# Attention's output projection for two tiles at once, as seven block products with streamed weights

## The chip, the core and the metric

The kernel runs on one core of a Trainium2 chip. The metric is the device time of one launch in microseconds (us); lower is better. All data are f32.

## The reference

The reference is four layers of a small network on `x`, 64 sequences of 32 positions with 512 features (2048 rows). The change touches the attention of the third layer only. Cut to that:

```python
q = rope(rmsnorm(x @ Wq.T)) ; k = rope(rmsnorm(x @ Wk.T)) ; v = x @ Wv.T   # 32 query heads, 8 key heads, 128 wide
k_all = concat(k_cache[pages], k) ; v_all = concat(v_cache[pages], v)      # 512 cached + 32 own positions
probs = softmax(where(valid, q @ k_all.T / sqrt(128), -1e30))
o = (probs @ v_all).reshape(64, 32, 32 * 128)
return o @ Wo.T                                                            # 4096 -> 512
```

The last line is what is computed in another way: for all 2048 rows, a product of a 2048 x 4096 matrix with a 4096 x 512 matrix.

## The kernel before, in words

The kernel runs layer 0 (`layer0`), layer 1 (`layer1`), and then `attention`, whose end (`Tail.run`) is the rest of layers 2 and 3. Attention goes over **32 steps**: two halves of the heads (`HALVES`, 16 query heads and 4 key heads each), and in each half 16 tiles of 128 rows, which are four sequences of 32 positions. A step has 16 **turns** (`per`), one for each sequence and key head. In a turn TensorE transposes the probabilities of the turn (`turned`), computes the scores of two turns later (`start`, `scores`, L791), and multiplies values by probabilities (`values`, tile `po`). VectorE and ScalarE do the softmax of a turn (L796 mask, scale and maximum; L798 exponential; L800 reciprocal; L803 division), so that the result is there two turns on.

The other work on TensorE stands in **slots**, two in each turn (0 to 31), written out by hand. These are the projections of the next step (`Projection.product`: keys `pk`, values `pv`, four groups of queries `pq`, each in two parts; then `turned`, the transposes after the rotation) and the output product of the step before (`Output.product`, tile `py`). The order of TensorE is that of the program text (`on_pe`); the orders of the other engines and of the DMA queue of SyncE (SP) are laid out by a scheduler from the same text. POOL adds and multiplies in the rotation (L694, L695) and issues the gathers of values (`load_values`, L662); SP issues the keys, 16 pages of 64 KB for each sequence (`load_keys`, `load_by` L98), whose page numbers it reads from DRAM into registers (`numbers`, L93).

A tile's heads are collected in `oT` (128 x 16 heads x 128 positions), which `own_part` fills for two sequences at a time (L839). The output product of a tile is 16 matmuls, one for each head of the half, with `oT` as weights and 512 columns of `wo` moving, in eight blocks of two matmuls in slots 18 to 31 (1 to 15 in the last step). The weights `wo` of a half (16 x 512 per partition, 32 KB) stay in SBUF. VectorE takes the sum out of PSUM (L768; in the second half L770 adds `y_before`, what the first half has left in DRAM). PSUM tiles of projections and outputs share the tag `mm` with two buffers; the small transposes share `tq` with one. The weights of the second half are loaded in steps 14 and 15 (`weights`, `output_weights`). After the last step the last tile's output product stands alone, and then `Tail.run` begins.

Of the kernel before, what the change touches and what calls it, by code (L numbers as in the profile page):

```python
# [60 lines left out]
class Common:  # L61
# [26 lines left out]
    def numbers(self, src, n):  # L88


        nc = self.nc
        with self.tc.issue_after(self.last_load) if self.last_load else nullcontext():
            _, values = nc.values_load_multi_w_load_instructions(  # L93
                src, engines=[mybir.EngineType.SP], min_val=0, max_val=n - 1)
        return values

    def load_by(self, dst, src):
        self.last_load = self.nc.sync.dma_start(dst, src).ins  # L98
# [458 lines left out]
class Known:  # L557


    def __init__(self, c, kp):  # L560
        tc, nc, a = c.tc, c.nc, c.a
        half = HD // 2
        with tc.tile_pool(name="l2_setup", bufs=1) as scratch:
# [10 lines left out]
            for h in range(HALVES):  # L574
                t = kp.tile([P, B * L // P], I32, name=f"v_rows{h}")
                nc.vector.tensor_scalar(t, rows_f, float(h), None, ALU.add)
                self.rows.append(t)
            lens_i = c.load(scratch, "lens", [P, B], a["lens"].to_broadcast([P, B]), I32)
# [13 lines left out]
def attention(c, known, x_in, y_part, y_out, tail):  # L592
# [13 lines left out]
    with ExitStack() as outer:  # L606
# [14 lines left out]
              "q": wp.tile([P, KC, HQP * HD], F32, name="wq"),  # L621
              "o": op.tile([P, HQP, D], F32, name="wo")}
# [21 lines left out]
        kts = {}  # L644
# [4 lines left out]
        def load_keys(h, b):  # L649
            pages = c.numbers(a["pages"][0:1, b * NPP:(b + 1) * NPP], PAGES)  # L650
            for n in range(NPP):
# [46 lines left out]
        class Projection:  # L698


            def __init__(self, h, T, w):
                self.h, self.T, self.w = h, T, w
                self.r, self.acc = {}, {}

# [19 lines left out]
            def product(self, what, u):  # L724

                n, g = (what, 0) if what in ("k", "v") else ("q", what)
                if what == "v" and u == 0:
# [23 lines left out]
        class Output:  # L751


            def __init__(self, h, T, oT, w):
                self.h, self.T, self.oT, self.w = h, T, oT, w

            def product(self, u):
                if u == 0:
                    self.acc = ps.tile([P, D], F32, tag="mm", bufs=2, name="py")
                    if self.h:  # L760
                        self.before = c.load(wk, "y_before", [P, D], y_part(self.T))
                part(self.acc, [(self.oT[:, n, :], self.w["o"][:, n, :]) for n in (2 * u, 2 * u + 1)],
                     u == 0, u == HQP // 2 - 1)
                if u < HQP // 2 - 1:
                    return
                y = wk.tile([P, D], F32, name="y")
                if self.h == 0:
                    nc.vector.tensor_copy(y, self.acc)  # L768
                else:
                    nc.vector.tensor_tensor(y, self.acc, self.before, ALU.add)  # L770
                self.y = y

            def store(self):
                nc.sync.dma_start((y_out if self.h else y_part)(self.T), self.y)
# [69 lines left out]
        def weights(h, what):  # L844
# [4 lines left out]
            nc.sync.dma_start(ws[n][:, :, g * D:(g + 1) * D],  # L849
                              a[f"W{n}T"][:, at:at + D].rearrange("(k p) n -> p k n", p=P))  # L850

        def output_weights(h, u):

            at = (h * HQP + 4 * u) * HD
            nc.sync.dma_start(ws["o"][:, 4 * u:4 * (u + 1), :],
                              a["WoT"][at:at + 4 * HD].rearrange("(n p) o -> p n o", p=P))
# [13 lines left out]
        def keys_of(i):  # L870
            if i < len(turns):
# [3 lines left out]
                load_keys(h, b)  # L875
# [16 lines left out]
        oTs, stores = {0: qp.tile([P, HQP, P], F32, name="oT")}, []  # L892
# [34 lines left out]
        with tc.issue_after(c.last_load):  # L927
            for u in range(HQP // 4):
                output_weights(0, u)
        for s, (h, T) in enumerate(steps):  # L930
            if s:
                oTs[s] = qp.tile([P, HQP, P], F32, name="oT")
            slots = [[] for _ in range(2 * per)]
            if s == 0:
                slots[0].append(partial(projections[0].turned, 2))
                slots[2].append(partial(projections[0].turned, 3))
                slots[2].append(partial(own_keys, 0, 1, projections[0].kT))
            if s + 1 < len(steps):
                p = projections[s + 1]
                for what, at in zip(("v", "k") + GROUPS,  # L940
                                    ((1, 2), (3, 4), (6, 7), (8, 10), (11, 13), (14, 16))):
# [388 lines left out]
```

## Time and profile before

| what | us |
|---|---|
| median of 3 runs (lowest to highest) | 3682.45 (3680.71 to 3685.24) |
| profiled execution, its own time | 3681.84 |
| its span, first to last instruction | 3679.8 |
| TensorE (PE) busy / weight loads (PEld) busy | 3631.7 / 2523.7 |
| VectorE (DVE) / ScalarE (ACT) / GpSimd (POOL) busy | 1805.6 / 1316.3 / 1254.1 |
| attention's steps, about | 1081 to 3495 |
| a step in the middle (32 of them) | about 73 |

The page gives busy times and the chain of work that ended last, followed back from the last instruction. Other views answer queries on the same execution: the waits of an engine (who waited for whom: us in total, times, longest), the chain in order of time (start, length, what), the timeline of an engine, groups of instructions, and windows (busy time of every engine in a stretch). PE records two entries for each f32 matmul. A busy record of PE can overlap the next, so paces are read from the chain in order of time or from starts in the timeline.

### The profile page before, as it was taken

How to read it: one execution, taken by the hardware profiler on the slowest of the kernel's cores; microseconds unless marked ns; L12 is line 12 of the kernel's file. 1: busy time of each engine (PE TensorE's matmuls, PEld its weight loads, DVE VectorE, ACT ScalarE, POOL GpSimd, SP SyncE). 2: the span in 40 equal slices, each digit the busy share in tenths (PEclk: the TensorE clock that was granted, in tenths of full speed). 3: DMA queues.
4: the chain of work that ended last, by engine and by line, in shares of the span. 5: the costliest groups of instructions: out<-in, count | busy, mean ns of one | idle time of the engine just before them, and what ended most of it. 6: DMA issues, size and time to landing. Idle time of an engine off the chain costs nothing.

```text
span 3679.8 us, 62184 instructions
## 1 busy us (share of the span) xinstructions
PE 3631.7 (99%) x18752; PEld 2523.7 (69%) x18752; DVE 1805.6 (49%) x4815; ACT 1316.3 (36%) x3014; POOL 1254.1 (34%) x1265
## 2 busy tenths in 40 slices
PE   8999999999999999999999999999999999999999
PEld 3444788888867776777777776777777777777755
DVE  5452222222236655565556655566555655566423
ACT  1111111111125444444444444444444444444411
POOL 0112100000035444544445444444444444454222
PEclk9999999999999999999999999999999999999999
DMA  5014211111144444344443355544444344444521
GB/s 209 23 35 162 92 44 60 44 47 34 37 141 134 124 122 122 117 116 116 123 122 118 115 184 179 165 132 119 123 123 125 117 123 122 129 120 123 160 68 61
DMA packets 410062, 407.70 MB, mean 111 GB/s; under 512 B 49954, under 2 KB 322338, under 8 KB 409730
## 3 DMA queue, kind: packets, MB, share of 16 engines
q1 hardware_dynamic: 363010, 251.65, 22.5%
q0 software_dynamic: 44416, 147.88, 13.2%
q10 hardware_dynamic: 2304, 4.20, 0.3%
q8 instruction: 153, 2.51, 0.3%
q14 instruction: 179, 1.47, 0.1%
HBM read 382.57 MB, written 20.97 MB: 110 GB/s over the span
## 4 chain that ended last, share of the span: by engine, by line
PE 89%; SPq 1%; DMA 0%; DVE 0%; issue 0%; ACT 0%; POOL 0%; ACTq 0%; POOLq 0%; DVEq 0%
PE po L640 14%; PE sc L791 13%; PE pq L640 12%; PE py L640 12%; PE gate_up L311 10%; PE prT_ps L635 6%; PE pz L311 5%; PE po L1100 3%; PE pv L640 3%; PE pk L640 3%; PE po L311 2%; PE qkT_ps L635 2%; PE pd L247 1%; PE ph L122 1%; SPq L93 0%
## 5 line engine op out<-in xcount | busy, mean ns | idle before, releaser
L662 POOL DMA_INDIRECT vt<-in_v_rows,v_rows x512 | 500.7, 978 | 816.7 <-PE po L640 708.8
L640 PEld LDWEIGHTS po<-prT,vt 128*128 128x128 f32 x4096 | 530.1, 192 | 183.7 <-issue 178.0
L796 DVE CUSTOM_DVE_ANT_0 pr<-sc,mask 128x544 f32<-128x544 f32 x512 | 369.2, 721 | 458.7 <-PE sc L791 457.5
L798 ACT ACTIVATE pr<-pr,low 128x544 f32<-128x544 f32 x512 | 383.4, 749 | 540.7 <-DVE low L796 536.4
L791 PE MATMUL sc<-kt,qT 128*128 128x288 f32 (+1 forms) x2048 | 555.1, 394 | 5.2 <-ACT qT L748 2.4
L640 PE MATMUL po<-prT,vt 128*128 128x128 f32 x4096 | 540.8, 275 | 1.6 <-ACT prT L809 1.6
L791 PEld LDWEIGHTS sc<-kt,qT 128*128 128x128 f32 x2048 | 369.2, 191 | 180.8 <-issue 106.9
L640 PE MATMUL py<-wo,oT 128*128 128x512 f32 x1024 | 480.3, 593 | 0.7 <-ACT oT L839 0.7
L640 PE MATMUL pq<-wq,xT 128*128 128x512 f32 x1024 | 480.9, 593 | 0.0
L809 ACT COPY prT<-prT_ps 128x512 f32<-128x512 f32 x512 | 298.5, 583 | 272.6 <-PE prT_ps L635 269.4
L803 DVE TENSOR_SCALAR pr<-pr,low 128x512 f32<-128x512 f32 x512 | 364.5, 712 | 16.7
L635 PE MATMUL prT_ps<-ident,pr 128*128 128x128 f32 x2048 | 310.9, 275 | 1.3 <-DVE pr L803 1.3
L640 PEld LDWEIGHTS py<-wo,oT 128*128 128x128 f32 x1024 | 192.6, 191 | 137.5 <-issue 125.6
L640 PEld LDWEIGHTS pq<-wq,xT 128*128 128x128 f32 x1024 | 182.8, 191 | 129.9 <-issue 125.1
L800 DVE RECIPROCAL low<-low 128x1 f32<-128x1 f32 x512 | 83.5, 163 | 360.6 <-ACT pr L798 359.6
L635 PEld LDWEIGHTS prT_ps<-ident,pr 128*128 128x128 f32 x2048 | 237.7, 141 | 9.1 <-issue 1.5
L126 POOL TENSOR_TENSOR rs<-rs,minus_half 128x4 f32<-128x4 f32 x160 | 166.2, 1039 | 167.4 <-DVE rs L678 166.1
L694 POOL TENSOR_TENSOR rot<-rot,swapped 128x512 f32<-128x512 f32 x160 | 202.7, 1267 | 1.0
L801 ACT ACTIVATE own_pr<-pr,low 128x32 f32<-128x32 f32 x512 | 164.2, 321 | 106.3 <-DVE low L800 104.2
L695 POOL TENSOR_TENSOR rot<-rot,rs 128x512 f32<-128x512 f32 x160 | 177.1, 1107 | 8.0
L395 DVE TENSOR_TENSOR sg<-sg,gate_up 128x256 f32<-128x256 f32 (+1 forms) x88 | 37.1, 421 | 277.3 <-ACT sg L394 277.3
L677 DVE TENSOR_REDUCE rs<-squares 128x4 f32<-128x512 f32 x160 | 109.6, 685 | 118.9 <-ACT squares L675 116.3
(208 smaller groups left out, 4649.8 us busy)
## 6 DMA issues: line engine op xcount, KB each, us to landing
kt<-in_kT SPq DMA_DIRECT2D x2048, 64.0 KB
xt<-x SPq DMA_DIRECT2D x48, 256.0 KB
wq<-in_WqT SPq DMA_DIRECT2D x12, 1024.0 KB
A<-in_A SPq DMA_DIRECT2D x64, 152.0 KB
sets<-in_cond0T SPq DMA_DIRECT2D x32, 256.0 KB
vt<-in_v_rows,v_rows POOLq DMA_INDIRECT x512, 3.7
wo<-in_WoT SPq DMA_DIRECT2D x8, 1024.0 KB
y<-y SPq DMA_DIRECT2D x32, 256.0 KB
```

The costliest lines, as they stand in the source:

```text
L126: self.nc.gpsimd.tensor_tensor(t, t, self.minus_half[:, :n], ALU.pow)
L311: c.on_pe(nc.tensor.matmul(out, lhsT, rhs, start=start, stop=stop))
L635: c.on_pe(nc.tensor.transpose(pt[:, m, :], piece, c.ident))
L640: c.on_pe(nc.tensor.matmul(out, lhsT, rhs, start=first and i == 0, stop=last and i == len(pairs) - 1))
L662: nc.gpsimd.indirect_dma_start(out=vts[b % 2][:, n, :], out_offset=None, in_=a["v_rows"], in_offset=bass.IndirectOffsetOnAxis(ap=rows[h][: ...
L694: nc.gpsimd.tensor_tensor(r, r, tmp, ALU.add)
L695: last = nc.gpsimd.tensor_tensor(r, r, rs.unsqueeze(2).to_broadcast([P, REP, HD]), ALU.mult)
L791: c.on_pe(nc.tensor.matmul(sc[:, lo + n * PSIZE:lo + m * PSIZE].rearrange("p (n k) -> p n k", k=PSIZE), q, kt[:, n:m, g, :], start=True, s ...
L796: nc.vector.tensor_tensor_reduce(pr[:, :NK], sc[:, lo:lo + NK], masks[h, b], -SCALE, 3.0e38, ALU.add, ALU.min, low[:, 0:1])
L798: nc.scalar.activation(pr[:, :NK], pr[:, :NK], AF.Exp, bias=low[:, 0:1], scale=-1.0, accum_out=low[:, 1:2])
L803: nc.vector.tensor_scalar(pr[:, :L], pr[:, :L], low[:, 2:3], None, ALU.mult)
L809: nc.scalar.copy(prT, pt)
```

## The change

The output of two neighbouring tiles is formed together. Let the tiles' rows be A1 and A2 (`oT` of two steps), each cut in its heads: 8 heads and 8 heads, so that A is 2 x 2 blocks of 128 rows x 1024. `Wo` of the half is cut in 2 x 2 blocks of 1024 x 256. Instead of eight block products, seven are computed, from sums and differences of blocks (Winograd's form of Strassen's scheme), and y is put together from the seven:

- Sums of blocks of `Wo` (four for each half) are made by VectorE in steps 0 and 1 (`sum_up`), and stored in DRAM (`sums`).
- Sums of blocks of `oT` are made for each pair: two by POOL (`first_sums`, 1024 elements each; by VectorE after the last step), two by VectorE in place between products (`next_sum`, in halves of 512).
- Weights come in pieces of 128 x 4 x 256 (0.5 MB), 14 for a pair, through four buffers (`wo_tile`, `wo_piece`, `next_wo`); the load of a piece is put into the slot after the block that released its buffer (`later`).
- A product has two blocks of 4 matmuls with 256 columns. A pair has 14 blocks, spread over the slots of the two steps that follow the pair; steps 0 and 1 have none, and the last pair's stand after the last step.
- The projections' slots are spread anew, with two plans (even and odd steps), and values come last in odd steps. In steps 14 and 15 the loads of the second half's weights move one slot.
- `oT` has three buffers, and `oTs` of a pair are kept until its products are done. y is put together by ScalarE (2 copies of 256), VectorE (5 additions of 256) and POOL (2 additions of 256, in the second half 2 of 512 with `y_before`).
- The page numbers are put into a table in SBUF once, held between their bounds there (`Known.pages`); `numbers` reads them from it, and the bounds are not looked at again on SP. A sequence's keys are issued in four parts over three slots.

The diff, cut to its core:

```diff
     def load_by(self, dst, src):
-        self.last_load = self.nc.sync.dma_start(dst, src).ins
+        with self.tc.issue_after(self.last_load) if self.last_load else nullcontext():
+            self.last_load = self.nc.sync.dma_start(dst, src).ins
...
-        def load_keys(h, b):
-            pages = c.numbers(a["pages"][0:1, b * NPP:(b + 1) * NPP], PAGES)
-            for n in range(NPP):
+        def load_keys(h, b, parts=range(4)):
+            if 0 in parts:
+                pages[:] = c.numbers(
+                    known.pages[b:b + 1, :], PAGES,
+                    skip_runtime_bounds_check_because="Known holds them between the bounds")
+            for n in range(parts[0] * NPP // 4, (parts[-1] + 1) * NPP // 4):
                 c.load_by(kts[h, b][:, n, :], a["kT"][ds(pages[n], 1), h].rearrange("a d f -> (a d) f"))
...
+        H = D // 2
+        KH = HQP // 2
+        QH = KH // 2
+        ORDER = (1, 2, 5, 6, 7, 3, 4)
+        ahead = 4
+        def wo_tile():
+            return op.tile([P, QH, H], F32, name="wo", bufs=ahead)
+        def sum_up(h, k):
+            w, t = [], []
+            def rows():
+                w.append(wo_tile())
+                for n in range(2):
+                    at = (h * HQP + n * KH + k) * HD
+                    c.load_by(w[0][:, 2 * n:2 * n + 2, :].rearrange("p a b -> p (a b)"),
+                              a["WoT"][at:at + HD, :])
+            def add():
+                t.append(wo_tile())
+                (b11, b12, b21, b22), (t1, t2, t3, t4) = ([v[0][:, n, :] for n in range(4)] for v in (w, t))
+                nc.vector.tensor_tensor(t1, b12, b11, ALU.subtract)
+                nc.vector.tensor_tensor(t3, b22, b12, ALU.subtract)
+                nc.vector.tensor_tensor(t2, b22, t1, ALU.subtract)
+                nc.vector.tensor_tensor(t4, b21, t2, ALU.subtract)
+            def store():
+                c.load_by(sums[h][:, k], t[0])
...
+        class Outputs:
...
+            def first_sums(self, engine):
+                self.o = [oTs.pop(2 * self.n + i) for i in range(2)]
+                (_, _), (o21, o22) = self.blocks = [(o[:, :KH, :], o[:, KH:, :]) for o in self.o]
+                self.s = qp.tile([P, KH, P], F32, name="o_sum", bufs=1)
+                engine.tensor_tensor(self.s, o21, o22, ALU.add)
+                engine.tensor_tensor(o21, self.blocks[0][0], o21, ALU.subtract)
+            def next_sum(self, m, u):
...
+                if m == 6:
+                    nc.vector.tensor_tensor(self.s[:, q], self.s[:, q], o11[:, q], ALU.subtract)
+                else:
+                    nc.vector.tensor_tensor(self.s[:, q], o12[:, q], self.s[:, q], ALU.subtract)
...
+            def product(self, i):
+                m, u = ORDER[i // 2], i % 2
...
+                if u == 0:
+                    self.acc = ps.tile([P, D], F32, tag="mm", bufs=2, name="py")[:, :H]
+                (o11, o12), (o13, o22) = self.blocks
+                lhs = {1: o11, 2: o12, 3: self.s, 4: o22, 5: self.s, 6: self.s, 7: o13}[m]
+                w = wos.pop(0)
+                part(self.acc, [(lhs[:, u * QH + n, :], w[:, n, :]) for n in range(QH)], u == 0, u == 1)
...
+        def slot(fs):
+            now = later[:]
+            del later[:]
+            for f in now[:2]:
+                f()
+            later[:] = now[2:]
+            for f in fs:
+                f()
...
-                for what, at in zip(("v", "k") + GROUPS,
-                                    ((1, 2), (3, 4), (6, 7), (8, 10), (11, 13), (14, 16))):
+                if s == 0:
+                    plan = (("v", 1, 2), ("k", 4, 6), (0, 8, 10), (1, 13, 16), (2, 17, 20), (3, 22, 25))
+                    then = (12, 16, 20, 25, 29)
+                elif s == 1:
+                    plan = (("k", 1, 3), (0, 5, 8), (1, 10, 12), (2, 16, 17), (3, 19, 21), ("v", 24, 27))
+                    then = (10, 13, 19, 24, 28)
+                elif even:
+                    plan = (("v", 1, 2), ("k", 3, 5), (0, 6, 8), (1, 9, 11), (2, 12, 13), (3, 15, 16))
+                    then = (10, 13, 17, 19, 21)
+                else:
+                    plan = (("k", 2, 4), (0, 5, 6), (1, 8, 9), (2, 11, 13), (3, 19, 20), ("v", 22, 24))
+                    then = (10, 12, 16, 19, 27)
...
-                slots[28].append(projections[s + 2].x)
+                slots[29 if s < 2 else 26].append(projections[s + 2].x)
                 if steps[s + 2][0] != h:
-                    for what, at in zip(("v", "k") + GROUPS, (3, 5, 8, 11, 14, 17)):
+                    for what, at in zip(("v", "k") + GROUPS, (4, 6, 9, 12, 15, 18)):
                         slots[at].append(partial(weights, steps[s + 2][0], what))
...
+            if n == 0:
+                for k in range(KH):
+                    for f, at in zip(sum_up(s, k), (0, 7, 9)):
+                        to_come.setdefault(s * 2 * per + 4 * k + at, []).append(f)
+            else:
+                out = outputs[n - 1]
+                if even:
+                    slots[4].append(partial(out.first_sums, nc.gpsimd))
...
+                    ats = (17, 19, 24, 27, 29, 31, 33, 36, 39, 41, 44, 47, 49, 52) if last_pair else \
+                        (17, 19, 20, 22, 24, 25, 27, 29, 31, 33, 48, 49, 60, 62)
...
-        for u in range(HQP // 2):
-            out.product(u)
+        out = outputs[-1]
+        out.befores()
+        out.first_sums(nc.vector)
+        for i in range(n_out):
+            out.product(i)
+            next_wo()
+            if i in (5, 7):
+                for u in range(2):
+                    out.next_sum(6 if i == 5 else 3, u)
         out.store()
```

Numbers of blocks' slots above 31 lie in the step after (48 is slot 16 of the odd step).

## The prediction

> **What bounds the kernel now.** First the page's busy times, then its chain of work.
>
> ```profile
> PE 3631.7 (99%) x18752; PEld 2523.7 (69%) x18752; DVE 1805.6 (49%) x4815; ACT 1316.3 (36%) x3014; POOL 1254.1 (34%) x1265
> ...
> PE 89%; SPq 1%; DMA 0%; DVE 0%; issue 0%; ACT 0%; POOL 0%; ACTq 0%; POOLq 0%; DVEq 0%
> PE po L640 14%; PE sc L791 13%; PE pq L640 12%; PE py L640 12%; PE gate_up L311 10%; PE prT_ps L635 6%; PE pz L311 5%; PE po L1100 3%; PE pv L640 3%; PE pk L640 3%; PE po L311 2%; PE qkT_ps L635 2%; PE pd L247 1%; PE ph L122 1%; SPq L93 0%
> ```
>
> TensorE carries the chain and the output product `py` is 12% of it. A busy PE can hide waiting, so next the waits of PE. From 1250 us to the end of attention they are these, and one of 0.2 us:
>
> ```profile
> PE sc L791 <- DMA kt<-in_kT: 1.6, 1, 1.6
> ...
> PE po L640 <- ACT prT L809: 1.6, 3, 0.8
> PE py L640 <- ACT oT L839: 0.7, 1, 0.7
> ```
>
> Less than 5 us of 2250: in attention TensorE is never kept waiting, and a PE microsecond taken out of it comes out of the time, unless a new wait appears. Its price is in the chain in order of time, which shows the pace from one matmul to the next, where the mean of a row (593 ns for 512 columns) includes overlap:
>
> ```profile
> 490.62 4.29 PE po L311 x10
> ...
> 503.63 12.95 PE gate_up L311 x60
> ...
> 2288.96 1.72 PE py L640 x4
> ```
>
> An f32 matmul leaves two records. A record of 512 columns takes 4.29/10 = 0.429 us (`py`: 1.72/4, the same), one of 256 columns 12.95/60 = 0.2158 us. `gate_up` is the right model for the new product: 256 columns, and new weights for each matmul.
>
> [...] a load of 191 ns disappears in a pace of 216 ns. [...] the trace has 1267 ns (L694) against some 690 ns (L263, 512 elements). [...]
>
> **The change part by part.**
>
> *The product.* Before: 1024 records x 0.429 = 439.3 us. After: 16 pairs x 7 products x 8 chunks = 896 matmuls, 1792 records x 0.2158 = 386.7 us. **-52.6 us**, all on the path. A block in a slot keeps its length (4 records of 0.429 = 1.72; 8 of 0.2158 = 1.73); there are just two fewer per pair.
>
> *The end.* The last pair runs as one stretch of 14 blocks x 1.73 = 24.2 us (in the sum above). Before, 32 records stood there:
>
> ```profile
> 3495.25 14.00 PE L640 MATMUL py<-wo,oT 128*128 128x512 f32 x32 [0.67 <-ACT oT L839]
> ...
> 3510.03 0.66 PE L1117 MATMUL yT_ps<-ident,y 128*128 128x128 f32 x4 [0.79 <-DVE y L770]
> ```
>
> The 0.7 us wait in front goes: products 1 and 2 read the earlier tile. The sums on VectorE (two of 1024 elements, twice the 691 ns of L263 each: 2.8 us) have 6.9 us of products 1 and 2 in front of them. The next sums come in halves, so half 0 is formed while half 1 of product 5 runs. Ten pieces of 0.5 MB must follow at 1.73 us each, with three blocks (5.2 us) between release and use. At the 391 GB/s of the fast window below a piece takes 1.3 us: hidden; at the 290 GB/s of 3400 to 3410 us it takes 1.8. Value -0.7 + 0.5, bounds -0.7 to +8.
>
> *Steps 0 and 1.* VectorE forms the weight sums: 32 additions of 256 a step at 0.42 us (L395) = 13.4 us. From this window (per step 42.1 us of VectorE) minus 0.7 for `y` plus 13.4 I get 54.8 us, in a step of 73.3 - 13.7 = 59.6 us: 92% busy. Behind the additions queue the softmax operations that TensorE needs (L796, L803).
>
> ```profile
> 1094.00:1098.00 4.00, 4.00 (x23) 2.76 (x22) 0.76 (x2) 1.80 (x6) 3.09 (x4) 1.00 1.04 391
> ...
> 1500.00:1573.00 73.00, 73.00 (x368) 51.03 (x366) 42.06 (x112) 33.99 (x78) 31.58 (x34) 1.00 0.41 123
> ```
>
> (Columns: stretch; busy us and count of PE, PEld, DVE, ACT, POOL; clock; DMA share; GB/s.) DMA is dense there too: per sequence, 14.9 us, 2.1 MB of keys and values plus 2.1 MB of rows and sums, 282 GB/s of at most 391. Not shown before; below by 0 (nothing gets faster), above by the excess if everything serialized, 13.4 us. I take **+4**.
>
> *Step 15.* Weights of half 1 are loaded in steps 14 and 15 both. In step 15 the reload of query group 3 (slot 18) now stands ahead of its use at slot 19; before, the use was at 14 and 16. SyncE issues it behind a piece that waits for the block of slot 17, so 0.5 + 0.25 + 1 MB must land: at 391 GB/s 4.6 us, plus 2 to 3 us to landing (gathers take 3.1 at least); `po`, transposes and scores cover 0.9 + 0.4 + 0.9 = 2.2. **+4** (2 to 7), once.
>
> *Spreading.* The transposes of `tq` (one PSUM buffer) stand closer: `xT` in slot 26, a query group in 27; a group in 13 or 21, then the own-probability transpose. After `qkT` the trace needs 0.89 us until the copy is usable (1080.88 to 1081.77); cover is 0.92 in the first case, 1.33 in the other, and ScalarE may be inside an exponential of 0.75. Some 0.1 us a step: **+3**, 0 to 10.
>
> *SyncE.* Per sequence it reads page numbers, then issues 16 keys, 0.525 us apart:
>
> ```profile
> L93 SPq TENSOR_LOAD <-in_pages_ptr x128: 837/859/5419, 803.2 to 3454.8; - x128
> L93 SPq TENSOR_LOAD <-in_pages x128: 1702/1816/4227, 804.8 to 3456.0; - x128
> ```
>
> 0.9 + 1.8 + 16 x 0.25 (bounds) + 8.4 = 15.1 of 18.3 us. The table in SBUF leaves one load (I keep 1.8) and no bounds: 10.2, plus two pieces at 0.5 = 11.2. Keys then need some 3.7 us to land (as a gather) and have 22 us from g = 1 to the start two turns before use. The one key wait, 1.6 us, followed loads of 5.42 and 3.60 us in that place: it should go, **-1.6**. A piece waits for the block one slot earlier, so keys behind it lose a slot (2.3 us) at most.
>
> *Hidden.* DMA: 3.7 MB more a step, 50 GB/s, 0.41 becomes 0.57. POOL: two additions of 1024 at 2 x 1267 ns, two of 256, two of 512 in half 1: 8.9 us per pair of 146; behind them wait the rotation of `k` (its block ends in slot 5, used in slot 10, 11 us) and gathers, which now wait 305 us per 1000 for PE. VectorE and ScalarE: some 4 us per pair for evacuations and half sums, in turns where VectorE is 58% busy. Each: 0, up to 5 in all if cover fails. The additional stores follow additions long done.
>
> Sum: -52.6 - 0.2 + 4 + 4 + 3 - 1.6 = **-43.4**. The profiled execution took 3681.84 us (span 3679.8): 3638.4. The median is 0.6 higher: **3639 us**.
>
> **The rivals.**
> - *No new wait*: the unknown terms are 0, -54.9: 3627.5. For it: in step 0 before, turns without a filler ran at 2.4 us each and still hardly waited. Against: VectorE had no additions then. 0.22.
> - *The first steps give way*: VectorE's and DMA's queues both fill, each step loses 10 us: 3655. For it: 92%; against: the rows of keys and additions come spread over four slots. 0.12.
> - *Slower*: head-of-line waiting at SyncE. If DMA moves small-row traffic at only 160 GB/s, the 3.0 MB of a sequence (keys, values, pieces) takes 18.8 us where TensorE needs 17.9: 0.9 us x 120 sequences = +108, minus 53: 3738. It decides below 168 GB/s (3.0/17.9), and loses all gain below 164. Against: 0.41 of the engines moved 123, so full ones move 300. 0.03.
> - *It doesn't do what it says*: if weight loads of the short matmuls aren't hidden, a record takes 0.245 us (439.3/1792) and nothing is gained: 3682. Against: 160 records of `gate_up` in a row at 0.22. 0.03.
> - Main case, 0.60.
>
> **How the numbers follow.** The time is the main case's. Its range: -54.9 with all unknowns at their best, 3627; high, the upper bounds of end, first steps, step 15 and spreading at once would be -53.3 + 8 + 13.4 + 7 + 10 = -15, which is unlikely together; 3662 holds the first-steps case and leaves out the two worst. What a measurement can tell from no change is 0.2%, 7.4 us. Faster: 0.60 + 0.22 + 0.12 = 0.94; same 0.03; slower 0.03.
>
> **What would show it.** `py` in the new profile: 1792 records, 256 columns, pace 0.216, some 10.6% of the span. Waits of PE: a wait of `pq` for `wq` once, of 2 to 7 us; waits for `pr` or `low` only between 1080 and 1200 us; waits of `qkT_ps` or `own_prT_ps` under 0.5 us each. SyncE without `in_pages_ptr`. DMA share near 0.57 in the middle. It would be wrong if waits of `sc` for `kt` or of `py` for `wo` recur in every pair, or if `py` steps wider than 0.22 us.

## The result, and the profile after

| | before | changed |
|---|---|---|
| median of 19 runs each (us) | 3681.9 | 3673.84 |
| lowest to highest | 3679.14 to 3687.68 | 3667.17 to 3679.21 |
| profiled execution, its own time | 3681.84 | 3676.43 |
| its span | 3679.8 | 3674.4 |

The ratio is 0.9974, 95% interval 0.9967 to 0.9981: faster by 8 us, where 43 were forecast. In the profiled executions the gain is 5.4 us. The product and the end gave the 53 us that were forecast of them, and some nine tenths of that, 47.4 us, was lost again in longer steps. This part shows where.

The page's busy times and the chain of work of the changed kernel:

```profile
PE 3600.2 (98%) x19520; PEld 2671.7 (73%) x19520; DVE 1916.2 (52%) x4996; ACT 1296.3 (35%) x3046; POOL 1371.8 (37%) x1343
...
PE 89%; DVE 5%; DMA 2%; ACT 1%; SPq 1%; issue 1%; POOL 0%; DVEq 0%; ACTq 0%; POOLq 0%
PE po L652 13%; PE sc L887 12%; PE pq L652 11%; PE gate_up L313 10%; PE py L652 9%; PE prT_ps L647 6%; PE pz L313 5%; PE po L1244 3%; PE ph L124 3%; PE pk L652 3%; PE pv L652 3%; DVE own_vt L685 2%; PE pd L249 2%; PE po L313 2%; PE qkT_ps L647 2%; PE py L204 1%
```

`py` is smaller, 9% in place of 12%, as meant. But VectorE and DMA, which had 0% of the chain, now have 5% and 2%, and a single line of VectorE, the copies of a tile's own values (L685), has 2%. So the waits come next. For the whole execution, PE's longest list by releaser:

```profile
PE py L204 <- DVE w L200: 10.7, 2, 10.1
PE pq L652 <- DMA wq<-in_WqT: 10.2, 1, 10.2
PE py L652 <- DMA wo<-wo_sums: 5.8, 3, 3.2
PE ph L124 <- DVE z L262: 5.4, 2, 2.9
PE qkT_ps L647 <- ACT xT L739: 4.2, 15, 0.3
PE sc L887 <- DVE low L892: 3.8, 3, 2.0
PE transposed L119 <- ACT routed L246: 3.5, 2, 1.9
PE sc L887 <- DMA kt<-in_kT: 3.4, 2, 2.7
PE prT_ps L647 <- DVE pr L899: 3.1, 2, 1.8
PE xT_ps L348 <- issue: 2.8, 1, 2.8
PE qkT_ps L647 <- POOL rot L711: 2.2, 1, 2.2
```

The lines at L204, L124, L119 and L348 belong to layers 0 and 1 and were there before. The other seven sum to 32.7 us. The steps lose more than that, so waits alone don't account for the loss. The lengths of the steps do: they are read from the timeline, where a step ends with the second `po<-own_prT,own_vt` of its tile. "Planned" takes the 75.8 us of a regular step before (measured here; the prediction reckoned with 73.3), minus 13.7 for its 32 output records, plus 1.725 us for each block that the new plan puts there.

| step (us) | before | planned | changed | lost |
|---|---|---|---|---|
| 0 and 1, from the first product with values | 138.4 | 124.6 | 142.7 | 18.1 |
| 2 | 75.8 | 77.6 | 78.6 | 1.0 |
| even ones with 9 blocks | 75.8 | 77.6 | 77.6 | 0 |
| odd ones with 5 blocks (13 of them) | 75.8 | 70.7 | 71.6 | 0.9 each, 11.7 |
| 14 | 76.1 | 77.6 | 80.3 | 2.7 |
| 15 | 78.0 | 70.7 | 84.1 | 13.4 |
| 30 | 75.4 | 72.0 | 72.0 | 0 |
| 31 | 60.9 | 60.9 | 63.9 | 3.0 |

The losses sum to 49.9 us, 47.4 more than the 2.5 that the kernel before lost in steps 14 and 15. Blocks in the steps save 31 x 13.73 - 15 x 14 x 1.725 = 63.4 us, and the stretch after them costs 10.2 more: -63.4 + 47.4 + 10.2 = -5.8, against -5.4 measured.

### The profile page after: what moved, and what is told of

Read it like the earlier page. It is cut to its first block, busy times and chain, and to the rows that moved or that the text cites. A ratio compares the mean times of both kernels' runs of the same rounds, so it can differ in the third digit from the quotient of the medians.

```text
span 3674.4 us, 60317 instructions
## 1 busy us (share of the span) xinstructions
PE 3600.2 (98%) x19520; PEld 2671.7 (73%) x19520; DVE 1916.2 (52%) x4996; ACT 1296.3 (35%) x3046; POOL 1371.8 (37%) x1343
## 4 chain that ended last, share of the span: by engine, by line
PE 89%; DVE 5%; DMA 2%; ACT 1%; SPq 1%; issue 1%; POOL 0%; DVEq 0%; ACTq 0%; POOLq 0%
PE po L652 13%; PE sc L887 12%; PE pq L652 11%; PE gate_up L313 10%; PE py L652 9%; PE prT_ps L647 6%; PE pz L313 5%; PE po L1244 3%; PE ph L124 3%; PE pk L652 3%; PE pv L652 3%; DVE own_vt L685 2%; PE pd L249 2%; PE po L313 2%; PE qkT_ps L647 2%; PE py L204 1%
## 5 line engine op out<-in xcount | busy, mean ns | idle before, releaser
L652 PEld LDWEIGHTS po<-prT,vt 128*128 128x128 f32 x4096 | 533.4, 192 | 96.7 <-issue 75.8
L652 PE MATMUL pq<-wq,xT 128*128 128x512 f32 x1024 | 482.5, 594 | 10.2 <-DMA wq<-in_WqT 10.2
L899 DVE TENSOR_SCALAR pr<-pr,low 128x512 f32<-128x512 f32 x512 | 329.5, 643 | 14.9
L896 DVE RECIPROCAL low<-low 128x1 f32<-128x1 f32 x512 | 83.3, 163 | 341.0 <-ACT pr L894 337.1
L652 PE MATMUL py<-wo,oT 128*128 128x256 f32 x1024 | 241.4, 379 | 0.0
L128 POOL TENSOR_TENSOR rs<-rs,minus_half 128x4 f32<-128x4 f32 x160 | 169.1, 1057 | 163.4 <-DVE rs L694 159.4
L710 POOL TENSOR_TENSOR rot<-rot,swapped 128x512 f32<-128x512 f32 x160 | 205.3, 1283 | 5.9 <-DVE swapped L707 4.7
L685 DVE COPY own_vt<-v 32x128 f32<-32x128 f32 x512 | 174.8, 341 | 35.8 <-PE po L652 25.6
L652 PE MATMUL py<-wo,o_sum 128*128 128x256 f32 x768 | 182.8, 381 | 5.9 <-DMA wo<-wo_sums 5.8
```

The lines of the kernel that those rows point to most:

```text
L128: self.nc.gpsimd.tensor_tensor(t, t, self.minus_half[:, :n], ALU.pow)
L652: c.on_pe(nc.tensor.matmul(out, lhsT, rhs, start=first and i == 0, stop=last and i == len(pairs) - 1))
L685: nc.vector.tensor_copy(own_vts[b % 2][g * S:(g + 1) * S, g % 2, :], v[j * S:(j + 1) * S, g * HD:(g + 1) * HD])
L710: nc.gpsimd.tensor_tensor(r, r, tmp, ALU.add)
L899: nc.vector.tensor_scalar(pr[:, :L], pr[:, :L], low[:, 2:3], None, ALU.mult)
```

## Experiments

The experiments ran on three chips, the kernel before beside each group of them. It took 3703 to 3715 us there (medians), not the 3682 above; which chip that was measured on is not on record. So a time is compared with another of the same chip or by its ratio to before, and step lengths carry the argument. In what was expected of a run, theory A is the explanation under test, and the rival or theory B is the one that it is weighed against.

**The second load of the weights, left out.**

```diff
-                if steps[s + 2][0] != h:
+                if even and steps[s + 2][0] != h:
```

> The second half's weights are loaded in step 14 alone; step 15's load of the same data is left out (nothing else changes, the output neither). Theory A: the wait of 10.2 us of a query projection for wq in step 15, and the half clock of about 3.6 us behind it, come from that second load alone: step 15 falls from 84.1 us to 71 or 72 us, and the time by 11 to 15 us. Rival: DMA is simply full there (pieces, keys and the tail of step 14's loads), and the wait moves to the next transfer, keys or pieces: the time falls by less than 4 us, and a wait for kt or wo over 5 us stands near 2260 us.

3666.76 us, 0.9909 of before (0.9893 to 0.9924). Step 15 takes 71.4 us in place of 84.1, step 14 77.6, and no wait for `wq` is left. Of the changed kernel, first SP's timeline, then PE's windows (busy us and count of PE, PEld, DVE, ACT, POOL, then clock, DMA share, GB/s), then the chain in order of time:

```profile
2249.28 0.98 SPq L100 DMA_DIRECT2D wq<-in_WqT  x2
2252.55 3.01 SPq L100 DMA_DIRECT2D wo<-in_WoT  x2
2255.61 0.50 SPq L85 DMA_DIRECT2D xt<-x  x1
2256.16 0.43 SPq L100 DMA_DIRECT2D wq<-in_WqT  x1
```

```profile
2245.00:2257.00 12.00, 12.00 (x84) 10.51 (x84) 10.22 (x22) 5.35 (x13) 7.28 (x7) 1.00 0.72 239
2257.00:2267.00 10.00, 0.66 (x3) 0.20 (x2) 2.72 (x9) 2.25 (x7) 0.00 (x0) 0.75 1.07 364
2267.00:2272.00 5.00, 4.16 (x7) 1.99 (x8) 0.00 (x0) 0.00 (x0) 0.00 (x0) 0.50 0.33 95
2272.00:2277.00 5.00, 5.00 (x30) 3.89 (x29) 0.79 (x2) 1.77 (x3) 0.00 (x0) 0.97 0.28 94
```

```profile
2256.16 11.64 DMA wq<-in_WqT
...
2267.84 3.78 PE pq L652 x4
```

So theory A held. The prediction had the order right: the reload of group 3 is issued last, at 2256.16, behind the pieces. It had the landing wrong: 11.6 us from issue, where its sum gives 6.6 to 7.6 (4.6 for the bytes in front and 2 to 3 to land). It counted 1.75 MB in front; the windows show the DMA engines full (a share of 1.07) at 364 GB/s for 10 us, 3.6 MB. The sizes of the packets in the trace tell the parts: 1.05 MB are pieces, two of them where the sum had one; 1.65 MB are the weights of `wq` and a tile of `x`; 0.55 MB are gathered values and 0.38 MB keys, which the sum left out. And the wait has a tail: the granted clock is 0.50 from 2262.02, inside the wait, to 2272.26, over the first 4.4 us of TensorE's work behind the wait, and the four records there take 3.78 us in place of 1.72.

**Steps 0 and 1: additions or DMA?** First without the additions, with all the traffic:

```diff
             def add():
-                t.append(wo_tile())
...
-                nc.vector.tensor_tensor(t4, b21, t2, ALU.subtract)
+                t.append(w[0])
```

> Left out: the 64 additions that form the weight sums in steps 0 and 1; the rows themselves are stored as sums, so all the loads, stores and pieces stay. Theory A: VectorE loses the 18 us in steps 0 and 1 (its additions of two SBUF inputs take up to 2.3 us instead of 0.42 beside POOL's, and the softmax queues behind them): the time falls by 14 to 19 us, the steps 0 and 1 take about 62 us each, and the waits for pr and low in them go. Rival B: the 16 MB of rows and sums in DMA are the cause (late keys, late values): the time stays within 3 us, and the steps stay at 70 us.

3662.15 us, 0.989 of before (0.9875 to 0.9905). From the first product with values to the end of step 1 it takes 127.7 us in place of 142.7 (142.9 and 142.6 in two other runs on the same chip that leave the sums as they are). So 15.0 of the 18.1 us go with the additions, and with them the waits for `pr`; for `low` 1.4 us are left. Theory A holds. Then the counterpart, additions without the traffic:

```diff
             def rows():
-                w.append(wo_tile())
-                for n in range(2):
...
+                if not kept:
+                    for n in range(2):
+                        kept.append(wk.tile([P, D], F32, name="y_before", bufs=2))
...
             def store():
-                c.load_by(sums[h][:, k], t[0])
+                pass
```

> The counterpart: the 64 additions stay on VectorE in the same slots, but they read two tiles of rows that are loaded once, their results are not stored, and pieces are read from the weights where sums were read (left out: the sums' traffic of 16 MB and their values). Theory A (VectorE): within 4 us of the changed kernel, steps 0 and 1 still near 71 us. Rival B (DMA): the time falls by 12 to 18 us. If both this one and the one without additions gain half, the two share the loss.

3670.89 us, 0.9917 (0.9904 to 0.9931); steps 0 and 1 take 137.6 us. This is less of a control than was meant: with no row to wait for, the scheduler laid all 64 additions into step 0, so step 1 is short (63.0 us) and step 0 long. Against the plan of 124.6, additions alone cost 13.0 us and traffic alone 3.1; the 2.0 that are missing to 18.1 are within what two runs of the same steps differ by (138.9 to 142.9). The steps are 5 us shorter than with the changed kernel's sums on that chip (142.6 and 142.9), where theory A had 4 at most and rival B 12 to 18: nearer to A, but neither number was met.

How an addition costs more than its 0.42 us is in the timelines of the changed kernel, VectorE's first and then POOL's, same stretch:

```profile
1111.36 0.71 DVE L892 CUSTOM_DVE_ANT_0 pr<-sc,mask 128x544 f32<-128x544 f32 x1
...
1111.99 1.97 DVE L793 TENSOR_TENSOR wo<-wo 128x256 f32<-128x256 f32 x1
1113.89 0.41 DVE L794 TENSOR_TENSOR wo<-wo 128x256 f32<-128x256 f32 x1
1114.22 2.34 DVE L795 TENSOR_TENSOR wo<-wo 128x256 f32<-128x256 f32 x1
1116.49 0.15 DVE L896 RECIPROCAL low<-low 128x1 f32<-128x1 f32 x1
1116.60 0.56 DVE L796 TENSOR_TENSOR wo<-wo 128x256 f32<-128x256 f32 x1
1117.09 0.47 DVE L899 TENSOR_SCALAR pr<-pr,low 128x512 f32<-128x512 f32 x1
```

```profile
1112.39 1.28 POOL L710 TENSOR_TENSOR rot<-rot,swapped 128x512 f32<-128x512 f32 x1
1113.83 0.97 POOL L678 DMA_INDIRECT vt<-in_v_rows,v_rows  x1 [0.16 <-issue]
1114.81 1.06 POOL L711 TENSOR_TENSOR rot<-rot,rs 128x512 f32<-128x512 f32 x1
```

The two long additions end 0.3 and 0.7 us after POOL's addition and multiplication of the rotation (L710 and L711, which end at 1113.67 and 1115.87); the one that falls between them takes 0.41. The reciprocal and the division of the softmax (L896, L899) stand behind, and TensorE waits 1.8 us for `pr`. Each of the 11 that took over 0.5 us (0.56 to 2.34) ran beside L710, L711 or the products for the tables of the rotation (L731, 128 x 128 elements); the other 53 took 0.43 at most, four of them beside L710 for 0.2 to 0.3 us and 13 beside the small operation of POOL at L128 (128 x 4). All 64 together took 35.6 us in place of the 26.8 that they would take at 0.42. So the stretching is 8.8 us of VectorE's time, and VectorE is busy for some 54 of the 71 us of each of these steps. How much of the loss comes from the stretching, and how much from additions that stand in front of a softmax, is not shown.

A part of the loss is in TensorE's clock. In steps 0 and 1 it fell to half three times, each time for 3.41 us (busy columns and clock as above):

```profile
1159.50:1162.90 3.40, 3.40 (x17) 3.35 (x16) 0.65 (x2) 1.62 (x4) 0.00 (x0) 0.50 0.45 123
1197.10:1200.50 3.40, 3.40 (x20) 3.08 (x20) 1.92 (x6) 1.16 (x3) 2.51 (x3) 0.50 0.55 139
1231.20:1234.60 3.40, 3.40 (x16) 3.11 (x15) 1.95 (x7) 2.24 (x6) 0.00 (x0) 0.50 1.03 407
```

Each stretch stands behind a wait of TensorE of 2.0 to 2.7 us (2.19, 2.04 and 2.69); behind the shorter ones of 1.33 to 1.80 us in these steps the clock stayed at 1.00. The kernel before has 1.00 from 401 to 3680 us, and the run without additions has a mean of 0.997, where the changed kernel has 0.995. In step 15 the four records of `pq` took 3.57 us from the first start to the start of what follows at 0.50, where they take 1.72 at 1.00. By that factor of two, the work of a stretch of 3.41 us would take half of it at 1.00, so each costs about 1.7 us, an estimate, and the three 5.1 of the 18.1 us; TensorE's waits there are 12.5 us, where the kernel before had 2.1.

**Fewer additions in one place.** Sums in place, half 0's alone in steps 0 and 1, half 1's in steps 3 to 10:

```diff
-                for k in range(KH):
-                    for f, at in zip(sum_up(s, k), (0, 7, 9)):
-                        to_come.setdefault(s * 2 * per + 4 * k + at, []).append(f)
+                for k in range(s * KH // 2, (s + 1) * KH // 2):
+                    for f, at in zip(sum_up(0, k), (0, 7, 9)):
+                        to_come.setdefault(k * 8 + at, []).append(f)
...
+                if 3 <= s < 3 + KH:
+                    for f, at in zip(sum_up(1, s - 3), (0, 25, 29)):
+                        slots[at].append(f)
```

> The weight sums are formed in place, and spread: those of the first half alone in steps 0 and 1 (16 additions a step in place of 32, one tile for each in place of two), those of the second half in steps 3 to 10, one set of four additions in each, through the buffers of y_before, which are free then. Theory A (VectorE's queue gives way to additions that POOL stretches): with half of them, steps 0 and 1 lose 2 to 4 us each in place of 9, and four additions in a step of 71 to 78 us are hidden: the time falls by 9 to 14 us against the changed kernel on the same chip. Rival: any addition on VectorE beside POOL's rotation costs its stretched time wherever it stands: the loss moves into steps 3 to 10, some 1 us each, and the time falls by 0 to 5 us.

3703.13 us, 0.9976 (0.9966 to 0.9986); the changed kernel itself on the same chip:

> The changed kernel itself, unaltered, as the measure for the three others on the same chip. Expected: 0.996 to 0.998 of the kernel before; steps 0 and 1 together some 143 us from the first product with values, even steps 77.6, odd 71.6, step 15 about 84 us.

3679.48 us, 0.9916 (0.9903 to 0.9929): a larger gain than was expected, and the range was missed. Its steps are nearly those of the table (even ones of the first half up to 78.2, step 2 79.6, step 14 81.0, step 15 82.9; steps 0 and 1 138.9). The spread is 24 us slower than that, and neither theory had it. VectorE's timeline of the spread:

```profile
1108.39 0.08 DVE L893 DVE_READ_ACCUMULATOR2_ANT low<- 128x1 f32 x1
1113.35 1.84 DVE L793 TENSOR_TENSOR wo<-wo 128x256 f32<-128x256 f32 x1 [4.88 <-DMA wo<-in_WoT]
...
1115.71 0.15 DVE L897 RECIPROCAL low<-low 128x1 f32<-128x1 f32 x1
```

The scheduler put the addition ahead of the softmax's reciprocal, and its row had not landed: VectorE stood still for 4.88 us, and TensorE for 5.9 us with it. The same recurs in steps 3 to 11, where VectorE waits 21.0 us for rows in 8 waits; these steps are 16.5 us longer than the changed kernel's on this chip, and steps 0 and 1 10.7 longer. The rival had the place of the second loss, but not its size. A slot fixes TensorE's order, not VectorE's. So two things were changed: in steps 0 and 1 rows are asked for 6 slots earlier, and all additions are tied behind the division of the latest turn (those of half 1 and their stores also come two slots earlier).

```diff
+                with tc.issue_after(last_div[0]):
+                    subtract(b11, b12, b21, b22)
...
-                    for f, at in zip(sum_up(0, k), (0, 7, 9)):
-                        to_come.setdefault(k * 8 + at, []).append(f)
+                    for f, at in ((load_rows, max(s * 2 * per, first - 6)), (add, first + 5), (store, first + 9)):
+                        to_come.setdefault(at, []).append(f)
```

> The spread sums again, with what failed in them mended: rows are asked for 6 slots earlier in steps 0 and 1, and each set of additions is laid on VectorE behind the division of the turn's softmax, so that neither a late row of weights nor the additions stand in front of a softmax. Theory A (order in VectorE's queue, additions stretched in front of the softmax): steps 0 and 1 together 128 to 134 us from the first product with values, steps 3 to 10 as in the changed kernel, and the waits of VectorE for rows under 0.5 us: about 9 to 14 us under the changed kernel (which took some 3675 us). Rival (additions cost wherever they stand, and SyncE's longer list delays keys): no gain, or slower by up to 10 us.

3677.67 us, 0.9903 (0.9888 to 0.9918). Steps 0 and 1 take 132.1 us, in the range of theory A, and VectorE no longer waits for a row; but the rival's number, no gain, held for the time. Steps 3 to 11 together take 6 us more than in the next run, which has the changed kernel's sums and ran on the same chip (72.8 or 72.9 in three of them): the first product with values of a step waits there, 7.8 us in 8 waits. Most of what is won in front is lost behind. And is it the order or the number? The order alone:

```diff
                 t.append(wo_tile())
+                with tc.issue_after(last_div[0]):
+                    subtract()
```

> The changed kernel with one edit: each set of four weight-sum additions is laid on VectorE behind the division of the latest turn's softmax; their number (32 in each of steps 0 and 1), places in the slots, loads and stores stay. Theory A (their place in front of a softmax in VectorE's queue makes the loss): steps 0 and 1 together take 130 to 135 us from the first product with values, as with half of the additions, in place of 139 to 143: 5 to 10 us under the changed kernel. Theory B (their number and their stretched time make it): within 3 us of the changed kernel, 138 to 143 us.

3678.26 us, 0.9905 (0.989 to 0.992), steps 0 and 1 141.3 us: theory B. With the softmax first, TensorE still waits: for `low` (3.9 us in 3 waits there), for prT's copy, once for an addition itself. So it is the number of additions in these two steps, since half as many took 132.1 us, and not their place ahead of or behind one softmax.

**The odd steps.** The wait in slots 26 and 27 is in the list above (`qkT_ps` for the copy of `xT`, 0.3 us and 15 times; from start to start it is 0.44 more, 1.36 in place of 0.92 in step 5). The other 0.42 us is in slots 17 and 18, shown by VectorE's timeline in step 5:

```profile
1649.36 4.31 DVE L685 COPY own_vt<-v 32x128 f32<-32x128 f32 x4 [0.31 <-PE po L652]
1653.69 0.16 DVE L896 RECIPROCAL low<-low 128x1 f32<-128x1 f32 x1
1653.89 0.22 DVE L685 COPY own_vt<-v 32x128 f32<-32x128 f32 x1
...
1656.09 0.72 DVE L892 CUSTOM_DVE_ANT_0 pr<-sc,mask 128x544 f32<-128x544 f32 x1
```

Four copies take 4.31 us, where one takes 0.22: POOL rotates query group 2 from 1650.11 to 1653.57. It is so in the whole run: 14 of these copies overlap the addition L710 and took about 2.1 us each, 14 overlap the multiplication L711 and took 1.4 to 1.6. Of the 484 others two took 3.03 and 1.51 us, beside POOL's additions of blocks (L826, L827) and of `y_before` (L866), and none of the rest more than 0.48. Both were moved, the rotation away from the copies and the transposes by a slot:

```diff
-(2, 11, 13), ... then = (10, 12, 16, 19, 27)
+(2, 11, 12), ... then = (10, 12, 16, 19, 28)
```

> In odd steps from 3 on the second part of query group 2 stands in slot 12 in place of 13 (its rotation on POOL ends ahead of the copies of own values in slot 16 to 17), and the transposes of query group 3 in slot 28 in place of 27 (xT in slot 26 has the tq buffer copied out by then). Theory A: the 0.85 us that odd steps take over the sum of their matmuls are these two, 0.42 and 0.44 us, 14 times: the time falls by 9 to 13 us, odd steps take 70.7 to 70.9 us. Rival: the waits reappear a turn later, or the copies only meet another POOL operation: 0 to 4 us.

3684.13 us, 0.9944 (0.9931 to 0.9958), no gain in the odd steps: 71.6 us. Both gaps are gone. With the rotation elsewhere the same four copies take 1.07 us:

```profile
1651.21 1.07 DVE L685 COPY own_vt<-v 32x128 f32<-32x128 f32 x4
```

But a new gap of 0.82 us (0.93 from start to start, where 0.11 is usual) stands in slot 14, in PE's timeline:

```profile
1647.22 0.27 PE L647 MATMUL own_prT_ps<-ident,own_pr 128*128 128x128 f32 x1
...
1648.15 1.18 PE L887 MATMUL sc<-kt,qT 128*128 128x288 f32 x4 [0.65 <-DVE low L892]
```

The product ends a slot earlier, so VectorE does its rotation (L693 to L707, 2.0 us) ahead of the softmax of that turn. The rival held: the wait came back elsewhere. With group 2 left in its place and the single load of the weights:

```diff
+                if even and steps[s + 2][0] != h:
...
+                    then = (10, 12, 16, 19, 28)
```

> The changed kernel with the two edits that leave the sums alone: the second half's weights loaded in step 14 alone, and query group 3's transposes in slot 28 of odd steps. Theory A: step 15 71 to 72 us and odd steps 71.2 us: -12 to -15 and -6, together 17 to 21 us under the changed kernel. Rival: the transposes' wait moves to a softmax: -12 to -15.

3661.14 us, 0.9856 (0.9841 to 0.9871). Most odd steps take 71.1 or 71.2, step 15 71.0, and after step 1 PE no longer waits for the copy of `xT`. Step 14 has 82.3: it waits 2.2 us for a piece, and the block behind the wait takes 3.11 us in place of 1.89. On the same chip this is 17 us under the run `ordered`, whose time is that of the changed kernel: theory A.

**The page table alone**, in the kernel before (the lines that make the table are not shown).

```diff
...
-            pages = c.numbers(a["pages"][0:1, b * NPP:(b + 1) * NPP], PAGES)
+            pages = c.numbers(known.pages[b:b + 1, :], PAGES,
+                              skip_runtime_bounds_check_because="Known holds them between the bounds")
```

> The kernel before with one part of the change alone: the page numbers in a table in SBUF, held between their bounds there, so that SyncE reads no pointer and looks at no bounds. Theory A (SyncE wasn't on the path but for one key wait of 1.6 us): the same time within 3 us; a sequence's keys are issued in about 11 us in place of 15. Rival (SyncE's bounds held something up all along): faster by 5 us or more.

3700.6 us, 0.9967 (0.9954 to 0.998): 12 us faster than the kernel before on that chip. The rival's number held, theory A's didn't. To see where the kernel before spends more there, it was traced beside the experiments:

> The kernel before, unaltered, for its trace on this chip: its runs beside the experiments took 3703 and 3713 us, while those shown took 3682 us. Theory A: regular steps are longer than 75.8 us each by one small wait of TensorE in the same place in every step, some 0.6 to 1 us. Rival: the 20 to 30 us lie in layers 0 and 1, ahead of the first step.

3711.91 us, 0.9995 (0.9986 to 1.0003), span 3709.0, 29 us over the span shown. Its instructions are the same, in the same order. Ahead of the first product with values it is 3.3 us shorter, steps 0 and 1 are 6.1 longer, and steps 2 to 31 26.3: 15 of them take 76.3 or 76.4 in place of 75.8, and a few much more (15: 83.6 for 78.0, 31: 67.2 for 60.9, 16 and 17: 77.8). Theory A had the place, and in those 15 steps nearly the form, one wait of some 0.5 us in the same place of each; they make 7.4 us. PE's waits of that run:

```profile
PE po L640 <- ACT prT L809: 13.6, 7, 3.4
...
PE po L640 <- issue: 4.6, 18, 0.6
PE sc L791 <- DMA kt<-in_kT: 3.7, 2, 2.9
```

Some are put to nothing the profile shows. In the place of the small wait it is ScalarE that comes late. Its timeline in the trace with 3682 us, then in this one:

```profile
1460.16 0.58 ACT L839 COPY oT<-po 128x512 f32<-128x512 f32 x1 [1.53 <-PE po L640]
1460.75 0.58 ACT L809 COPY prT<-prT_ps 128x512 f32<-128x512 f32 x1
```

```profile
1464.65 0.59 ACT L839 COPY oT<-po 128x512 f32<-128x512 f32 x1 [2.15 <-PE prT_ps L635]
1466.84 0.59 ACT L809 COPY prT<-prT_ps 128x512 f32<-128x512 f32 x1 [1.60 <-PE sc L791]
```

The second copy follows the first at once in the one, and 1.60 us later in the other, with ScalarE idle; what holds it the profile doesn't show. With the page table, regular steps still take 76.3 us, and the 12 us come from the long ones (15: 76.3 for 83.6, 31: 63.7 for 67.2, 16, 17 and 5 some 2 us less each). So the place of the difference is known. Why the kernel before takes 30 us more in these runs and the changed one 5 stays open; that it is the chip is inferred, not shown.

**Together.** First the spread as it was at first, with the late rows, the single load and slot 28:

> Three things together: the spread sums, one load of the second half's weights (step 14 alone), and in odd steps from 3 on the transposes of query group 3 in slot 28 in place of 27 (group 2 stays). Theory A: -9 to -14 for the sums, -12 to -15 for the load, and 0.44 us for each of 15 odd steps, -6: together 27 to 35 us under the changed kernel on the same chip, some 0.989 to 0.991 of the kernel before. Rival: the transposes' wait only moves to a softmax wait, as it did with group 2 moved: 20 to 28 us.

3684.65 us, 0.9928 (0.9915 to 0.9942): 5 us slower than the changed kernel on the same chip, where the two numbers had 20 to 35 us faster; steps 0 and 1 take 148.9 us, and step 15 71.0. Now with the mended spread:

> The mended spread, the single load of the second half's weights, and query group 3's transposes in slot 28 of odd steps. Theory A: 25 to 33 us under the changed kernel (about 3645 to 3650 us, 0.980 to 0.990 of the kernel before on the same chip). Rival: what the spread gives in steps 0 and 1 is lost in steps 3 to 10: 16 to 20 us.

3659.38 us, 0.9846 (0.9833 to 0.986), 2 us from the run with the single load and slot 28 alone (3661.14, same chip): the rival held, the mended spread adds nothing that can be measured. The same with the weights' loads split, keys and groups 0 and 1 in step 14, the others in step 15:

```diff
-                    for what, at in zip(("v", "k") + GROUPS, (4, 6, 9, 12, 15, 18)):
+                    for what, at in (("k", 6), (0, 9), (1, 12)) if even else ((2, 1), (3, 6), ("v", 10)):
```

> The mended spread and the transposes in slot 28 as before, with the second half's weights loaded once and over two steps: keys and query groups 0 and 1 in step 14 (slots 6, 9, 12), groups 2 and 3 and values early in step 15 (slots 1, 6, 10). Theory A (in step 14 SyncE's list and DMA are full of 5 MB of weights ahead of the pieces): the wait for a piece of 1.7 to 2.2 us in step 14 goes, step 14 falls from 79.6 or 82.3 to 78 us, step 15 stays at 71 to 72: 2 to 4 us under the single load in step 14 (3659 us). Rival: a projection of step 15 waits for its weights again, 2 us or more, and the time is the same or longer.

3660.62 us, 0.9866 (0.9849 to 0.9883). Steps 14 and 15 take 78.2 and 71.0, with no wait for a piece or for weights there, as theory A said; the time is not measurably different. The three that hold the single load and slot 28 without the late rows (3661.14, 3659.38 and 3660.62 us) can't be told apart; all are faster than both kernels (0.9916 for the changed one).

## Why the prediction was wrong

By the terms of its sum, predicted and then measured, in us against before (step 15: 13.4 lost, less 0.6 of the 2.2 that the step lost before; the other 1.6 are the key wait, under SyncE):

| term | predicted | measured | step of it that failed |
|---|---|---|---|
| product | -52.6 | -53.0 | none |
| end | -0.2 | -0.2 | none |
| steps 0 and 1 | +4 | +19.1 (with step 2) | size, and the clock |
| step 15 | +4 | +12.8 | size, and the clock |
| spreading | +3 | +11.7 | size, and one of two mechanisms |
| pieces in steps 14 and 31 | 0 ("hidden") | +5.4 | the cover |
| SyncE | -1.6 | -1.6 | none |
| sum | -43.4 | -5.8 | |

*Product: right.* A block stepped by 1.73 us as foretold, and the likeness to `gate_up` held. Even steps came out at the planned 77.6.

*End: right.* PE's timeline after the last step, and the next layer's first transpose:

```profile
3478.98 7.17 PE L652 MATMUL py<-wo,oT 128*128 128x256 f32 x32
...
3489.76 3.69 PE L652 MATMUL py<-wo,o_sum 128*128 128x256 f32 x16 [0.16 <-DMA wo<-wo_sums]
...
3504.66 0.66 PE L1261 MATMUL yT_ps<-ident,y 128*128 128x128 f32 x4 [0.57 <-DVE y L860]
```

Ten pieces in a row cost one wait of 0.16 us; the 0.67 us in front is gone.

*Steps 0 and 1: the mechanism right, the size wrong.* The prediction saw VectorE nearly full, with the softmax queued behind the additions. Its work for VectorE, 54.8 us a step, was right: 53 to 54 were measured. What failed is the step from there to the cost. "13.4 us if everything serialized" is the additions of one step, while the term is for two steps, whose 64 additions make 26.8 us at the same 0.42; +4 was taken of it without a working. The 0.42 was taken from L395, an addition with one input in PSUM; here additions between SBUF tiles took 35.6 us, up to 2.34 each. And a TensorE wait was priced without the stretch of 3.41 us at 0.50 that three of them had behind them. Measured are 18.1 us, of which 15.0 go with the additions and 3.1 are there with the traffic alone. That is near the second rival's 10 us a step, which had only 0.12.

*Step 15: the order right, the queue in front of it short.* It counted 1.75 MB at 391 GB/s and got 4.6 us; 3.6 MB were moved while TensorE stood, with a second piece, values and keys among them. And it priced a wait by its length alone. In the trace of the changed kernel 0.50 is granted for 10.24 us around the end of the wait of 10.2 us, and for 3.41 us from 3425.96 in step 31, behind a wait of 3.2, where a block takes 3.06 us in place of 1.89. The length of a wait alone doesn't tell which: waits of 2.0 to 2.7 us in steps 0 and 1 were followed by 0.50, while after one of 2.4 us in step 14 the clock stayed at 1.00 and the next block took 1.99. In the run `load_turn` a block took 3.11 us after a wait of 2.2.

*Spreading: 0.1 us a step taken, 0.9 found, in odd steps only.* The tq buffer was named with the right pair of slots; its cover was short by 0.28 us, not by 0.1. The other half, copies of own values that take 1.4 to 2.1 us beside POOL's rotation, was not thought of: it was under "Hidden", where each engine's time was weighed by itself.

*Pieces: hidden in all regular steps, not in 14 and 31*, where SyncE issues weights (of half 1, of the tail) in the same slots: waits of 2.4 and 3.2 us. For step 14 the last run shows it: with these loads spread over two steps the wait is gone. For step 31 it is read from SyncE's list and was not tested. The prediction added up DMA for a regular step (0.57 of the engines, and the window from 2340 to 3400 us has just that) but not for those two.

```profile
2340.00:3400.00 1060.00, 1057.60 (x5980) 826.38 (x5979) 668.68 (x1698) 497.32 (x1184) 546.57 (x531) 1.00 0.57 174
```

*SyncE: right.* The pointer reads are gone, and a page read takes 1.0 us where 1.8 was kept (0.86 and 1.82 before):

```profile
L93 SPq TENSOR_LOAD <-pages x128: 967/1007/2702, 1063.3 to 3438.3; - x128
```

The key wait of 1.6 us in step 15 is gone; a new one of 2.7 us stands in step 1, among the losses there. That the page table alone gives 12 us in the kernel before was not foreseen; it is located, in the long steps, and not explained.

What was to show it held in part: one wait of `pq` for `wq`, but of 10.2 us in place of 2 to 7; `pr` and `low` only in steps 0 and 1; `qkT_ps` under 0.5 us each, except one of 2.2 us for POOL in step 0.

## What to carry to other kernels

Before giving VectorE more work in a stretch, look at what POOL does in that stretch, price the work by rows that ran beside POOL (here up to 2.34 us for an addition that took 0.42 elsewhere), and count all the steps that the term is for. Add up DMA for the exceptional steps (loads of new weights, first and last steps) and not only for the regular one, and look at the granted clock behind a wait of TensorE before pricing it at its length: here waits of 2.0 to 2.7 us in steps 0 and 1 were followed by 3.41 us at 0.50, some 1.7 us more each by the estimate above, though one of 2.4 in step 14 was not. When a hand-made order fixes one engine alone, check where the other engines' queues put the work that goes with it, since moving one operation by a slot took a wait away in one place and made an equal one in another.

## What the runs showed of the hardware

- Copies of 32 x 128 on VectorE, with one input, took longer beside POOL's two-input operations of 512 and 1024 elements: four took 4.31 us in place of 0.9, and 1.07 when the rotation stood elsewhere; single ones beside the rotation took 1.4 to 2.1 us, where 0.22 is usual. Additions of 128 x 256 between SBUF tiles took up to 2.34 us there, where 0.42 is usual.
- The granted clock fell to 0.50 for stretches of 3.41 us after waits of TensorE of 2.0 to 2.7 us (three times in steps 0 and 1) and of 3.2 us (step 31), and from 2262.02 to 2272.26, of which TensorE waited 5.8 us. After a wait of 2.4 us in step 14 it stayed at 1.00.
- The kernel before took 3682 us in the runs of the result and 3703 to 3715 in those beside the experiments, the changed one 3674 and 3679: a gain of 8 us here is one of 33 us there (0.9916 of before). The granted clock was 0.99 or more in all of them; that another chip is the cause is likely, but not shown.
